# A recommender kernel's user stage: fixed rings of tiles, shorter lags and another order of the steps

## The chip, the cores and the metric

The kernel runs on one core of a Trainium2 chip. The time is that of one execution on the device, in microseconds (us). The profile is one such execution, recorded by the hardware profiler. TensorE (PE in the profile; its weight loads are PEld), VectorE (DVE), ScalarE (ACT), GpSimd (POOL) and SyncE (SP) each work through a queue of their own, in order.

## What is computed

Cut to what matters, the reference is:

```python
near_full = concat([near_pois, pad_row])              # 50001 items x 32 neighbours
def neighbor_attn(E):                                 # E: 50001 x 32
    V = E[near_full]                                  # gather
    w = softmax(einsum('nd,nkd->nk', E, V) / sqrt(32))
    return einsum('nk,nkd->nd', w, V)
a_sus, a_inf = neighbor_attn(E_in), neighbor_attn(E_out)
h = concat([E_hist[history], a_sus[history], a_inf[history]])   # 16384 x 100 x 128
t = concat([E_tgt[target],  a_inf[target],  a_sus[target]])     # 16384 x 128
z = relu(einsum('bld,hd->blh', h * t[:, None, :], W1) + b1)     # hidden size 128
exp_A = exp(einsum('blh,h->bl', z, W2[0])) * ((history != target) & (history != 0))
attn = exp_A / sqrt(sum(exp_A, -1))
s = sum(h * attn[..., None])                          # one number
out = sigmoid(dot / norms)                            # of s and t, for each of the 16384
```

## The kernel before

There are two long stages, one after the other.

The **neighbour stage** (lines 109 to 238) computes the two attentions for every item and writes one row of 129 numbers for each item into a table in HBM (`table`: the row's sum, then its 128 numbers), and one row of 128 into `ttab`. Its 12512 gathers are indirect DMAs issued by GpSimd at line 144. The diff does not touch it.

The **user stage** (lines 240 to 399) takes 128 chunks of 128 users each. A chunk has 100 history items per user, taken in groups of `LG = 4`, so `NG = 25` steps to a chunk and 3200 steps in all. The order of every engine's queue is the order of the program text; a framework puts in the semaphore waits that the data needs. An instruction can carry a wait of its own; where it needs a further one, a separate waiting instruction is put before it on that engine's queue. For step s:

- `gather(s)`, line 306, GpSimd: four indirect DMAs, each of which brings one row of 129 numbers for 128 users, into a tile `h`. There are `HBUF = 20` such tiles, so gathers run ahead of the work by up to 20 steps. The gather of step s + 20 must wait until TensorE and VectorE have read the tile of step s.
- `turn(s)`, line 320, TensorE: four transposes of 128x128 into one PSUM tile `hT_ps`, from a pool of three.
- `times_target(s)`, line 325, VectorE: multiplies that tile by the target's transposed row into `xT` (pool of six); line 328 copies the four row sums to `hsum`.
- `hidden(s)`, line 337, TensorE: one matmul with W1 (two passes in the profile) into `z_ps` (pool of three); line 339, ScalarE: bias and relu into `z` (pool of six).
- `scored(s)`, line 345, TensorE: one matmul (two passes) that adds the step's scores into `bank`, one PSUM tile for a chunk.

Once for each chunk there come `target_rows` (one gather, line 270), `target_work` (lines 282 to 297), `weights` (line 351), `exponents` (lines 358 and 360: four transposes into a tile of the same pool as `hT_ps`, and an Exp) and `ended` (lines 367 to 370).

The loop runs the steps with lags of `LAG = 3`. In iteration s the order is gather(s), turn(s), times_target(s), hidden(s-3), scored(s-6), and then the work of a chunk. Of PSUM's eight banks three go to `hT_ps`, three to `z_ps` and two to `bank`.

Of the kernel before, what the change touches and what calls it, by code (L numbers as in the profile page):

```python
# [10 lines left out]
F32 = mybir.dt.float32  # L11
# [3 lines left out]
AF = mybir.ActivationFunctionType  # L15
ALU = mybir.AluOpType
AX = mybir.AxisListType

P = 128
# [4 lines left out]
D = 128  # L24
# [22 lines left out]
LAG = 3  # L47
M = 2
HBUF = 20

# [3 lines left out]
def kernel(  # L54
# [194 lines left out]
    with (  # L249
# [12 lines left out]
        rows, got, hT, xT, z = {}, {}, {}, {}, {}  # L262
# [15 lines left out]
        def target_work(c):  # L278
            u = users[c]
            t = u["t"]  # L280
            tT_ps = ps_t.tile([P, LG, P], F32, name="hT_ps")
# [17 lines left out]
        def gather(s):  # L299
            c, g = divmod(s, NG)  # L300
            rows[s] = u_h.tile([P, LG, W], F32, name="h")
            got[s] = []
            for q in range(LG):
                l = g * LG + q
                got[s].append(
                    nc.gpsimd.indirect_dma_start(  # L306
                        out=rows[s][:, q, :],
                        out_offset=None,
                        in_=table,
                        in_offset=bass.IndirectOffsetOnAxis(  # L310
                            ap=users[c]["hidx"][:, l : l + 1], axis=0
                        ),
                    )
                )

        def turn(s):
            c, g = divmod(s, NG)
            hT[s] = ps_t.tile([P, LG, P], F32, name="hT_ps")
            for q in range(LG):
                nc.tensor.transpose(hT[s][:, q, :], rows[s][:, q, 1:W], ident)  # L320

        def times_target(s):
            c, g = divmod(s, NG)
            xT[s] = u_x.tile([D, LG, P], F32, name="xT")
            nc.vector.tensor_tensor(  # L325
                xT[s], hT.pop(s), users[c]["tT"].to_broadcast([D, LG, P]), ALU.mult
            )
# [4 lines left out]
            for one in got.pop(s):  # L332
                tc.declare_no_dep(copy.ins, one.ins, reason="TensorE has read the row")

        def hidden(s):
            z_ps = ps_z.tile([HID, LG, P], F32, name="z_ps")
            nc.tensor.matmul(z_ps, w1T, xT.pop(s), start=True, stop=True)  # L337
            z[s] = u_z.tile([HID, LG, P], F32, name="z")
            nc.scalar.activation(z[s], z_ps, AF.Relu, bias=b1_sb)  # L339

        def scored(s):
            c, g = divmod(s, NG)
            if g == 0:
                users[c]["bank"] = ps_s.tile([NG, LG, P], F32, name="bank")
            nc.tensor.matmul(  # L345
                users[c]["bank"], pick[:, g, :], z.pop(s), start=g == 0, stop=g == NG - 1
            )
# [6 lines left out]
        def exponents(c):  # L354
            flat = users[c].pop("flat")
            score = ps_t.tile([P, LG, P], F32, name="hT_ps")
# [20 lines left out]
        for s in range(last + 2 * LAG + 6):  # L377
            c, g = divmod(s, NG)
            if s < last:
# [107 lines left out]
```

## Time and profile before

| | us |
|---|---|
| median of 3 runs | 36161.68 (36157.8 to 36170.7) |
| the profiled execution | 36158.99 |
| its span, first to last instruction | 36157.2 |
| neighbour stage, to the first gather of the user stage | about 17540 |
| user stage, to its last gather | about 18550 |
| GpSimd busy | 25713.0 (71% of the span) |
| TensorE matmuls busy | 9955.5 (28%) |
| VectorE busy | 6910.6 (19%) |
| ScalarE busy | 2692.6 (7%) |

A row of a group of instructions reads: line, engine, operation, output <- inputs, shapes, count | busy us, mean ns of one | idle us of that engine just before them, and what ended the idle time. A row of a timeline reads: start us, length us, engine, line, operation, shapes, count, and in brackets the engine's idle time before it with what ended it.

### The profile page before, as it was taken

Reading aid. Unit: us, or ns where it says so; the run is one execution under the profiler, and the core shown is the slowest. Engines: PE = TensorE matmul, PEld = TensorE weight load, DVE = VectorE, ACT = ScalarE, POOL = GpSimd, SP = SyncE. Lnnn points to the kernel's source line nnn. Section 1 sums busy time; section 2 is a strip of 40 time slices with the busy share of each in tenths; the row PEclk is TensorE's granted clock in tenths of the full one; section 3 lists DMA queues with packets and bytes.
Section 4 is the critical chain, followed back from the end, with each engine's and each line's share of the span. In section 5 each row is a group of like instructions: output and inputs, shape, how many; then the busy total and the mean of one; then the engine's idle time right before and its main releaser. Section 6 shows DMA issues by size and latency. Waiting matters only on the chain.

```text
span 36157.2 us, 104181 instructions
## 1 busy us (share of the span) xinstructions
PE 9955.5 (28%) x26243; PEld 3219.9 (9%) x26243; DVE 6910.6 (19%) x9965; ACT 2692.6 (7%) x5700; POOL 25713.0 (71%) x25446
## 2 busy tenths in 40 slices
PE   0000000000000000000255555555555555555555
PEld 0000000000000000000011111111111111111111
DVE  2222222222222222222111111111111111111111
ACT  0000000000000000000011111111111111111111
POOL 7777777777777777777666666666666666666666
PEclk9999999999999999999877777777777777777777
DMA  1111111111111111111111111111111111111111
GB/s 42 29 27 27 27 28 29 27 27 27 28 29 28 27 27 28 27 29 25 40 47 47 47 47 47 47 46 47 47 47 47 46 47 46 47 47 47 46 46 43
DMA packets 1027956, 1362.32 MB, mean 38 GB/s; under 512 B 559904, under 2 KB 614432, under 8 KB 1027360
## 3 DMA queue, kind: packets, MB, share of 16 engines
q0 software_dynamic: 814080, 1265.42, 14.4%
q10 hardware_dynamic: 151056, 51.51, 0.8%
q1 hardware_dynamic: 62224, 38.72, 0.4%
q8 instruction: 218, 3.57, 0.0%
q14 instruction: 378, 3.10, 0.0%
HBM read 1315.31 MB, written 51.50 MB: 38 GB/s over the span
## 4 chain that ended last, share of the span: by engine, by line
POOL 37%; another core or an unknown queue 29%; PE 18%; issue 13%; DVE 2%; ACT 1%; DMA 0%; POOLq 0%; SPq 0%; ACTq 0%; DVEq 0%
POOL v L144 37%; PE z_ps L337 7%; PE bank L345 6%; PE hT_ps L320 5%; DVE xT L325 1%; ACT z L339 1%; DVE hsum L328 0%; DMA v<-in_egeo_dram,nidx 0%; PE hT_ps L358 0%; POOL h L306 0%; PE hT_ps L282 0%; ACT flat L351 0%; DVE tT L284 0%; DVE keep L293 0%
## 5 line engine op out<-in xcount | busy, mean ns | idle before, releaser
L306 POOL DMA_INDIRECT h<-table,hidx x12800 | 12107.2, 946 | 6300.4 <-issue 3830.4
L144 POOL DMA_INDIRECT v<-in_egeo_dram,nidx x12512 | 13484.1, 1078 | 4013.5 <-issue 3964.1
L325 DVE TENSOR_TENSOR xT<-hT_ps,tT 128x512 f32<-128x512 f32 x3200 | 2198.7, 690 | 15477.9 <-remote 9681.0
L282 PE MATMUL hT_ps<-ident,t 128*128 128x128 f32 x128 | 46.3, 362 | 17780.0 <-DMA t<-ttab,tidx 17522.1
L337 PE MATMUL z_ps<-xT,w1T 128*128 128x512 f32 x6400 | 4177.9, 741 | 1833.5 <-ACT z L339 1463.2
L320 PE MATMUL hT_ps<-ident,h 128*128 128x128 f32 x12800 | 2520.1, 328 | 5521.0 <-DVE xT L325 3984.9
L345 PE MATMUL bank<-z,pick 128*25 128x512 f32 x6400 | 3978.8, 709 | 0.0
L339 ACT ACTIVATE z<-z_ps,b_sb 128x512 f32<-128x512 f32 x3200 | 2149.8, 687 | 15996.4 <-remote 7924.9
L159 DVE TENSOR_TENSOR prod<-v,own_ps 128x4096 f32<-128x4096 f32 x196 | 864.4, 4410 | 12916.3 <-DMA v<-in_egeo_dram,nidx 12850.6
L320 PEld LDWEIGHTS hT_ps<-ident,h 128*128 128x128 f32 x12800 | 1621.4, 163 | 8660.4 <-DVE xT L325 4994.7
L282 PEld LDWEIGHTS hT_ps<-ident,t 128*128 128x128 f32 x128 | 19.1, 149 | 17919.3 <-issue 17586.5
L176 ACT ACTIVATE ex<-sc,top 128x32 f32<-128x32 f32 x782 | 227.8, 291 | 16993.6 <-DVE top L170 12332.7
L192 DVE TENSOR_TENSOR wv<-v,ex 128x1024 f32<-128x1024 f32 x782 | 1378.3, 1875 | 315.9 <-ACT ex L176 299.5
L337 PEld LDWEIGHTS z_ps<-xT,w1T 128*128 128x128 f32 x6400 | 1175.1, 230 | 2056.4 <-ACT z L339 1647.9
L166 DVE TENSOR_REDUCE sc<-prod 128x128 f32<-128x4096 f32 x196 | 864.4, 4410 | 6.7
L200 DVE TENSOR_REDUCE att<-wv 128x128 f32<-128x4096 f32 x196 | 864.1, 4409 | 6.0
L345 PEld LDWEIGHTS bank<-z,pick 128*25 128x25 f32 x6400 | 433.4, 109 | 3095.3 <-issue 3095.3
L328 DVE COPY hsum<-h 128x4 f32<-128x4 f32 x3200 | 568.9, 178 | 0.0
L358 PE MATMUL hT_ps<-ident,flat 25*128 25x25 f32 x512 | 65.8, 249 | 1051.5 <-ACT flat L351 714.5
L270 POOL DMA_INDIRECT t<-ttab,tidx x128 | 121.1, 946 | 65.9 <-issue 64.1
L358 PEld LDWEIGHTS hT_ps<-ident,flat 25*128 25x128 f32 x512 | 51.5, 170 | 1190.1 <-ACT flat L351 777.2
L176 ACT ACTIVATION_READ_ACCUMULATOR ex<-sc,top 128x1 f32 x782 | 146.0, 187 | 0.0
(55 smaller groups left out, 855.7 us busy)
## 6 DMA issues: line engine op xcount, KB each, us to landing
h<-table,hidx POOLq DMA_INDIRECT x12800
v<-in_egeo_dram,nidx POOLq DMA_INDIRECT x12512
table<-row ACTq DMA_DIRECT2D x22, 1096.5 KB
own<-in_egeo_dram SPq DMA_DIRECT2D x23, 544.0 KB
row<-in_ehist_dram SPq DMA_DIRECT2D x23, 544.0 KB
ttab<-in_etgt_dram ACTq DMA_DIRECT2D x1, 12500.0 KB
ttab<-row ACTq DMA_DIRECT2D x22, 544.0 KB
hidx<-in_history_dram SPq DMA_DIRECT2D x32, 200.0 KB
```

What stands on the lines that cost most here:

```text
L144: nc.gpsimd.indirect_dma_start(out=v[:, m, k].rearrange("p t d -> p (t d)"), out_offset=None, in_=egeo, in_offset=bass.IndirectOffsetOnAxi ...
L159: nc.vector.tensor_tensor(prod[:, 0:n].rearrange("p m k t d -> p m k (t d)"), v.rearrange("p m k t d -> p m k (t d)"), own_ps[:, 0:n].to_b ...
L166: nc.vector.tensor_reduce(sc[:, 0:n].rearrange("p m t k -> p m k t"), prod[:, 0:n], AX.X, ALU.add)
L192: nc.vector.tensor_tensor(wv[:, m, t].rearrange("p d k -> p k d"), subs[b]["v"][:, m, :, t, :], ex[:, m, t, :].rearrange("p (k o) -> p k o ...
L200: nc.vector.tensor_reduce(att[:, 0:n], wv[:, 0:n], AX.X, ALU.add)
L306: nc.gpsimd.indirect_dma_start(out=rows[s][:, q, :], out_offset=None, in_=table, in_offset=bass.IndirectOffsetOnAxis(ap=users[c]["hidx"][: ...
L320: nc.tensor.transpose(hT[s][:, q, :], rows[s][:, q, 1:W], ident)
L325: nc.vector.tensor_tensor(xT[s], hT.pop(s), users[c]["tT"].to_broadcast([D, LG, P]), ALU.mult)
L328: copy = nc.vector.tensor_copy(users[c]["hsum"][:, g * LG : (g + 1) * LG], rows.pop(s)[:, :, 0:1].rearrange("p q o -> p (q o)"),)
L337: nc.tensor.matmul(z_ps, w1T, xT.pop(s), start=True, stop=True)
L339: nc.scalar.activation(z[s], z_ps, AF.Relu, bias=b1_sb)
L345: nc.tensor.matmul(users[c]["bank"], pick[:, g, :], z.pop(s), start=g == 0, stop=g == NG - 1)
```

## The change

Only the user stage changes.

- The pools of `hT_ps`, `z_ps`, `xT` and `z`, from which each step took a tile, become lists of tiles that are allocated once and used in turn: `hT` has `TB = 2` (three before), `z_ps` has `ZP = 3` (three), `xT` has `XB = 4` (six), `z` has `ZB = 4` (six).
- The tile that `target_work` and `exponents` took from the pool of `hT_ps` comes from a pool of its own with one tile, `e_ps`.
- For two writes of one engine to the same tile of a ring, and for VectorE's read after the first three of the four transposes, the framework is told that no wait is needed (the engine's own order covers it, or the wait for the fourth transpose).
- The lags: hidden runs `LH = 2` steps behind turn (3 before), scored `LS = LH + ZP = 5` steps behind (6 before).
- The order in an iteration: gather(s), scored(s-5), hidden(s-2), turn(s), times_target(s), the work of a chunk.

The gathers, their 20 tiles, and the number and shapes of all matmuls, transposes and elementwise instructions stay as they are.

```diff
-LAG = 3
+TB = 2
+XB = 4
+ZP = 3
+ZB = 4
+LH = 2
+LS = LH + ZP
...
-        tc.tile_pool(name="u_x", bufs=6) as u_x,
-        tc.tile_pool(name="u_z", bufs=6) as u_z,
+        tc.tile_pool(name="u_r", bufs=1) as u_r,
...
-        tc.tile_pool(name="ps_t", bufs=3, space=bass.MemoryType.PSUM) as ps_t,
-        tc.tile_pool(name="ps_z", bufs=3, space=bass.MemoryType.PSUM) as ps_z,
+        tc.tile_pool(name="ps_r", bufs=1, space=bass.MemoryType.PSUM) as ps_r,
+        tc.tile_pool(name="ps_e", bufs=1, space=bass.MemoryType.PSUM) as ps_e,
...
+        hT = [ps_r.tile([P, LG, P], F32, name=f"hT{i}") for i in range(TB)]
+        z_ps = [ps_r.tile([HID, LG, P], F32, name=f"z_ps{i}") for i in range(ZP)]
+        xT = [u_r.tile([D, LG, P], F32, name=f"xT{i}") for i in range(XB)]
+        z = [u_r.tile([HID, LG, P], F32, name=f"z{i}") for i in range(ZB)]
+
+        def in_order(one, other):
+            tc.declare_no_dep(one.ins, other.ins, reason="one engine writes both in its order")
...
         def turn(s):
...
+                turned[s, q] = nc.tensor.transpose(
+                    hT[s % TB][:, q, :], rows[s][:, q, 1:W], ident
+                )
+                if s >= TB:
+                    in_order(turned[s, q], turned[s - TB, q])
...
         def times_target(s):
...
+            times[s] = nc.vector.tensor_tensor(
+                xT[s % XB], hT[s % TB], users[c]["tT"].to_broadcast([D, LG, P]), ALU.mult
+            )
+            for q in range(LG - 1):
+                tc.declare_no_dep(
+                    times[s].ins, turned[s, q].ins, reason="TensorE turns them in order"
+                )
+            if s >= XB:
+                in_order(times[s], times.pop(s - XB))
...
         def hidden(s):
+            first[s] = nc.tensor.matmul(
+                z_ps[s % ZP], w1T, xT[s % XB], start=True, stop=True
+            )
+            if s >= ZP:
+                in_order(first[s], first.pop(s - ZP))
+            second[s] = nc.scalar.activation(z[s % ZB], z_ps[s % ZP], AF.Relu, bias=b1_sb)
+            if s >= ZB:
+                in_order(second[s], second.pop(s - ZB))
...
-        for s in range(last + 2 * LAG + 6):
+        for s in range(last + LS + 6):
...
                 gather(s)
+            if 0 <= s - LS < last:
+                scored(s - LS)
+            if 0 <= s - LH < last:
+                hidden(s - LH)
+            if s < last:
                 turn(s)
                 times_target(s)
-            if 0 <= s - LAG < last:
-                hidden(s - LAG)
-            if 0 <= s - 2 * LAG < last:
-                scored(s - 2 * LAG)
...
-            done, left = divmod(s - 2 * LAG - NG, NG)
+            done, left = divmod(s - LS - NG, NG)
```

More of the change, by code (lines that the diff above doesn't have):

```diff
@@ L261 @@
         users, hists = {}, {}
-        rows, got, hT, xT, z = {}, {}, {}, {}, {}
+        got, turned, times, first, second = {}, {}, {}, {}, {}
+        rows = {}
+        hT = [ps_r.tile([P, LG, P], F32, name=f"hT{i}") for i in range(TB)]
[4 more added lines that the diff above has]
+            tc.declare_no_dep(one.ins, other.ins, reason="one engine writes both in its order")
         def history_of(i):
@@ L280, in target_work @@
             t = u["t"]
-            tT_ps = ps_t.tile([P, LG, P], F32, name="hT_ps")
+            tT_ps = ps_e.tile([P, LG, P], F32, name="e_ps")
             nc.tensor.transpose(tT_ps[:, 0, :], t, ident)
@@ L331, in times_target @@
             )
-            for one in got.pop(s):
-                tc.declare_no_dep(copy.ins, one.ins, reason="TensorE has read the row")
+            for q in range(LG):
+                tc.declare_no_dep(
+                    copy.ins, got.pop((s, q)).ins, reason="TensorE has read the row"
+                )
         def hidden(s):
[L336 to L339, printed above, removed]
+            first[s] = nc.tensor.matmul(
[6 more added lines that the diff above has]
+                in_order(second[s], second.pop(s - ZB))
         def scored(s):
@@ L345, in scored @@
             nc.tensor.matmul(
-                users[c]["bank"], pick[:, g, :], z.pop(s), start=g == 0, stop=g == NG - 1
+                users[c]["bank"], pick[:, g, :], z[s % ZB], start=g == 0, stop=g == NG - 1
             )
@@ L355, in exponents @@
             flat = users[c].pop("flat")
-            score = ps_t.tile([P, LG, P], F32, name="hT_ps")
+            score = ps_e.tile([P, LG, P], F32, name="e_ps")
             for q in range(LG):
```

23 lines of the change are left out of this document (7 added, 16 removed).

## The prediction

> **What bounds the kernel now.** I read the page first: its span, the chain that ended last and the costliest groups.
>
> ```profile
> span 36157.2 us, 104181 instructions
> ...
> POOL 37%; another core or an unknown queue 29%; PE 18%; issue 13%; DVE 2%; ACT 1%; DMA 0%; POOLq 0%; SPq 0%; ACTq 0%; DVEq 0%
> ...
> L325 DVE TENSOR_TENSOR xT<-hT_ps,tT 128x512 f32<-128x512 f32 x3200 | 2198.7, 690 | 15477.9 <-remote 9681.0
> ...
> L337 PE MATMUL z_ps<-xT,w1T 128*128 128x512 f32 x6400 | 4177.9, 741 | 1833.5 <-ACT z L339 1463.2
> L320 PE MATMUL hT_ps<-ident,h 128*128 128x128 f32 x12800 | 2520.1, 328 | 5521.0 <-DVE xT L325 3984.9
> L345 PE MATMUL bank<-z,pick 128*25 128x512 f32 x6400 | 3978.8, 709 | 0.0
> ```
>
> In the user stage no compute engine is near full: TensorE's three groups sum to 10677 us, VectorE's multiplies to 2199 us, and this in a stage of some 18550 us. VectorE sat 15478 us before its multiplies, most of it for a releaser that the profile can't name, and TensorE sat 5521 us before its transposes, for VectorE. So I asked next what GpSimd does in that stage, by line and by tile.
>
> ```profile
> L306 POOL DMA_INDIRECT h<-table,hidx x12793 | 12100.6, 946 | 6294.7 <-issue 3828.5 <-PE hT_ps L320 1786.3 <-DMA h<-table,hidx 265.2
> ...
> L306 POOL DMA_INDIRECT h<-table,hidx x12793: 939/947/1037, 17539.7 to 36092.5; - x200
> ```
>
> The gathers run from 17539.7 to 36092.5, that is 18552.8 us, and only about 65 us of the span come after them. They set the stage's length: 12793 of them, and 127 of the target's rows. The timeline of GpSimd shows at what pace.
>
> ```profile
> 23541.99 0.95 POOL L306 DMA_INDIRECT h<-table,hidx  x1 [0.30 <-issue]
> 23549.27 0.95 POOL L306 DMA_INDIRECT h<-table,hidx  x1 [6.33 <-PE hT_ps L320]
> 23550.52 0.95 POOL L306 DMA_INDIRECT h<-table,hidx  x1 [0.30 <-DVE xT L325]
> ...
> 23593.16 0.95 POOL L306 DMA_INDIRECT h<-table,hidx  x1 [0.30 <-issue]
> 23601.38 0.94 POOL L306 DMA_INDIRECT h<-table,hidx  x1 [7.27 <-PE hT_ps L320]
> ...
> L306 POOL DMA_INDIRECT h<-table,hidx x28 | 26.5, 946 | 13.6 <-issue 7.3 <-PE hT_ps L320 5.4 <-DMA h<-table,hidx 0.6
> ...
> L306 POOL DMA_INDIRECT h<-table,hidx x36 | 34.1, 946 | 17.1 <-issue 8.7 <-PE hT_ps L320 7.2 <-DMA h<-table,hidx 0.6
> ```
>
> A gather starts every 1.25 us, 0.95 busy and 0.30 between, until all 20 tiles are full; then GpSimd stands for some 7 us until one is free. The last two rows count the gathers from one such pause to the next: 28 before the pause of 6.33 us, 36 (nine steps) before that of 7.27 us. In the whole stage the idle time beyond 0.30 us a gather is 6294.7 - 12793 x 0.30 = 2457 us; a pause exceeds 0.30 by 6.0 and 7.0 us here, so with 6.5 there are some 378 pauses, one in every 8.5 steps. Without any, the stage would be 2.4 ms shorter.
>
> Why the tiles come free late is seen on VectorE and TensorE in the cycle between these two pauses.
>
> ```profile
> 23547.76 0.69 DVE L325 TENSOR_TENSOR xT<-hT_ps,tT 128x512 f32<-128x512 f32 x1 [10.50 <-PE bank L345]
> 23548.44 0.68 DVE L325 TENSOR_TENSOR xT<-hT_ps,tT 128x512 f32<-128x512 f32 x1
> 23549.10 0.68 DVE L325 TENSOR_TENSOR xT<-hT_ps,tT 128x512 f32<-128x512 f32 x1
> 23549.77 0.68 DVE L325 TENSOR_TENSOR xT<-hT_ps,tT 128x512 f32<-128x512 f32 x1
> 23554.25 0.69 DVE L325 TENSOR_TENSOR xT<-hT_ps,tT 128x512 f32<-128x512 f32 x1 [3.71 <-PE hT_ps L320]
> 23556.86 0.69 DVE L325 TENSOR_TENSOR xT<-hT_ps,tT 128x512 f32<-128x512 f32 x1 [1.64 <-PE hT_ps L320]
> 23559.28 0.69 DVE L325 TENSOR_TENSOR xT<-hT_ps,tT 128x512 f32<-128x512 f32 x1 [1.56 <-PE hT_ps L320]
> 23568.30 0.69 DVE L325 TENSOR_TENSOR xT<-hT_ps,tT 128x512 f32<-128x512 f32 x1 [8.08 <-PE z_ps L337]
> 23587.90 0.69 DVE L325 TENSOR_TENSOR xT<-hT_ps,tT 128x512 f32<-128x512 f32 x1 [18.83 <-issue]
> 23599.87 0.69 DVE L325 TENSOR_TENSOR xT<-hT_ps,tT 128x512 f32<-128x512 f32 x1 [11.21 <-PE bank L345]
> ...
> 23548.51 1.12 PE L320 MATMUL hT_ps<-ident,h 128*128 128x128 f32 x4 [1.76 <-DVE xT L325]
> 23549.42 1.92 PE L337 MATMUL z_ps<-xT,w1T 128*128 128x512 f32 x2
> 23551.26 1.90 PE L345 MATMUL bank<-z,pick 128*25 128x512 f32 x2
> 23553.09 1.12 PE L320 MATMUL hT_ps<-ident,h 128*128 128x128 f32 x4
> 23554.00 1.26 PE L337 MATMUL z_ps<-xT,w1T 128*128 128x512 f32 x2
> 23555.19 1.04 PE L345 MATMUL bank<-z,pick 128*25 128x512 f32 x2
> ...
> 23558.58 0.65 PE L320 MATMUL hT_ps<-ident,h 128*128 128x128 f32 x4
> 23559.08 1.02 PE L337 MATMUL z_ps<-xT,w1T 128*128 128x512 f32 x2
> 23560.03 1.04 PE L345 MATMUL bank<-z,pick 128*25 128x512 f32 x2
> 23561.00 0.66 PE L320 MATMUL hT_ps<-ident,h 128*128 128x128 f32 x4
> 23563.42 0.66 PE L320 MATMUL hT_ps<-ident,h 128*128 128x128 f32 x4
> ```
>
> The cycle has a quick and a slow stretch. Up to 23559.28 a multiply starts as soon as its transposes end (turn at 23558.58 for 0.65 us, multiply at 23559.28). Then TensorE's completions reach VectorE late: the turn that ends at 23561.66 is used at 23568.30, the one that ends at 23564.08 at 23587.90, 24 us later. The next multiply comes at 23599.87, which is 5.76 us after GpSimd went silent (23593.16 + 0.95). In the cycle before, the first multiply came 4.82 us after the silence (23547.76, after 23542.94). So while gathers are issued TensorE's results are seen at about one step in 20 us, and when the issue stops they come through. What holds them up the trace doesn't show; that it goes with the gathers it does. Seven quick steps and two slow ones make the nine steps of the cycle.
>
> **The price of a pause.** From 28 to 36 gathers the silence before the first multiply grows from 4.82 to 5.76 us, about 0.118 us a gather: a backlog that is paid in any order of work. The rest belongs to the pause itself. Over the stage: 2457 us less 12920 x 0.118 = 932 us, or 2.5 us for each of 378 pauses. The ends: if the silence were all backlog, only the 1.5 us from multiply to gather, less 0.3, is the pause's own, 1.2 us; if none, 6.5. I take 2.5, for it agrees with the whole stage. So the change is worth what it does to the number of pauses, that is to the steps per cycle.
>
> **The ring of transposes, three tiles to two.** When a slow stretch ends, the first three multiplies (23547.76, 23548.44, 23549.10) take turns that TensorE had made before: its first new one starts at 23548.51. These are the ring's three tiles. With two there are two. And in the new order TensorE doesn't stand before a turn, but before hidden(s), which now needs the multiply and comes ahead of the turn. With the durations above: multiply s ends at 23548.45, hidden from 23548.51 to the next start 1.84 later, turn to 23551.47, third multiply at 23551.5; then scored (1.83), hidden at the higher clock (1.19) and turn (0.65), fourth multiply at 23554.98; then every 2.42 us, as from 23558.58 to 23561.00: 23557.40 and 23559.82. Before, seven multiplies were done by 23559.28; now six by 23559.82, if the quick stretch ends at the same time. I take that it does, since it goes with the gathers and not with TensorE's work: one quick step less.
>
> One step less frees four gathers fewer: the slow stretch is 5.0 us shorter, at 20 us a step a further 0.25 step, and so on: 1/(1 - 0.25) = 1.33 steps. 8.5 becomes 7.2 steps, 378 pauses become 444. 66 x 2.5 = **+165 us** (79 at 1.2, 429 at 6.5).
>
> The Trainium skill, Perfetto Trace Analysis, Optimization Strategy, says that a gap that repeats on an engine can mean too little SBUF or PSUM for the next tile. It speaks against shortening this ring. TensorE's 5521 us before its transposes, 3985 of them for VectorE's multiply, are such gaps, and the trace agrees; by the rule the ring costs time, as in the sum, and it names no amount.
>
> **The separate waits.** They are not among the busy instructions, so I bound them. On VectorE they can't cost time in a quick stretch: multiplies start 0.67 us apart there at a length of 0.68. ScalarE's relu isn't on this path while three z_ps tiles stay. On TensorE, scored at 23560.03 is followed by turn 0.97 later, while hidden is followed by scored after 0.95: some 0.02 us, 0.07 at most, against 2.42 a step. It counts only in the quick stretch, 6 x 0.07 = 0.4 us in 52. I take nothing. If a separate wait took a place among the completions that trickle, 17 to a step (eight weight loads, eight matmuls, one wait), the slow stretch would give 2.1 steps for 2, some 20 us in all, less than the 0.2% (72 us) that a measurement here can tell.
>
> **Order, xT and z rings, chunk tile.** xT of four is read two steps later by hidden, z of four three steps later by scored: slack of two and of one step against work of 0.69 us. The chunk's two uses of e_ps lie nine steps apart. Exponents follow the last scored by a little more TensorE work than before. All nothing. The gathers themselves, and the stage ahead, are as before. At the tail scored follows one step, 2.4 us, sooner.
>
> The sum is made on the profiled execution's own 36158.99 us (span 36157.2 and 1.8 around it; the median of the runs, 36161.68, is 2.7 above): + 165 + 0 - 2 gives 36322, with the 2.7 about **36325 us**.
>
> **The rivals.** *Not slower:* the quick stretch ends after so many completions, not after a time. Then seven steps are quick in either kernel, it only lasts longer, pauses stay 378, and the time is 36160. For it: every quick step puts the same number of completions into the line. Against: in this cycle the trickle begins ten gathers after GpSimd resumed, as long as a backlog that grows with gathers would need. It decides if a profile after shows seven quick steps. The Trainium skill, TensorE: Matmul & The Clock Gate, "The cost: per-tile semaphore tail", gives 26 ns for each completion signalled; by it transposes would never be seen late and the ring's length would cost nothing, the same 36160. The 24 us above speak against that rule here.
>
> *Faster:* the separate waits do belong to what clogs, and without them the quick stretch holds for one or two steps more. One step, the ring's loss paid: 8.5 + 1.33 = 9.8 steps, 326 pauses, -130 us: 36030; a second one 35930. Against: the bound above. For: three engines wait separately, and I see none of it.
>
> *Slower still:* TensorE stays at the lower clock after each slow stretch (1.92 us for a pair, not 1.02), since it now begins with one pair and a turn and waits again. Two quick steps go: 5.8 steps, 552 pauses, +435: 36595. For: pairs of 1.9 last until 23553 even with three turns in hand.
>
> *It doesn't do what it says:* the waits stay under another name; then the ring alone acts, which is the forecast.
>
> **How the numbers follow.** Forecast 0.42, not slower 0.22, faster 0.24, slower still 0.12. The forecast lies over the 72 us unless a pause costs 1.1 us or less, which I hold for unlikely. So faster by more than 0.2%: 0.25, within: 0.22, slower: 0.53. The range reaches from the faster case with one step, a little beyond, to the slower case: 36000 to 36600.
>
> **What would show it.** Right: GpSimd's idle time in the user stage rises by about 150 to 200 us; a cycle has 28 to 32 gathers; after a silence two multiplies start 0.7 apart and the third some 3 us later. Wrong: cycles of 36 gathers or more, or a gather pace other than 1.25 us. Matmul counts and lengths should not change.

## The result, and the profile after

| | before | after |
|---|---|---|
| median of 21 runs each | 36163.92 us | 36218.61 us |
| lowest to highest | 36136.88 to 36175.84 | 36200.41 to 36249.47 |
| profiled execution: span | 36157.2 us | 36207.1 us |
| its granted TensorE clock | 0.854 | 0.864 |

The changed kernel takes 1.0016 times as long, 95% interval 1.0009 to 1.0023: some 55 us slower. That is the side that the prediction took, at a third of its size (+165 us), and below the 72 us that it had set as the least that could be told; with 21 runs of each it could.

The page of the changed kernel: the span, and the groups that answer to those shown of before. GpSimd's gathers are L317 now, the transposes L328, the multiplication by the target L336, the two TensorE products L355 and L368.

```profile
span 36207.1 us, 98804 instructions
...
L317 POOL DMA_INDIRECT h<-table,hidx x12800 | 12076.4, 943 | 6387.1 <-issue 5175.1
...
L355 PE MATMUL z_ps<-xT,w1T 128*128 128x512 f32 x6400 | 4542.5, 798 | 8512.6 <-DVE xT L336 7742.9
L336 DVE TENSOR_TENSOR xT<-hT,tT 128x512 f32<-128x512 f32 x3200 | 2206.6, 691 | 15844.6 <-remote 10547.6
...
L368 PE MATMUL bank<-z,pick 128*25 128x512 f32 x6400 | 3896.7, 695 | 0.3 <-ACT z L360 0.3
...
L328 PE MATMUL hT<-ident,h 128*128 128x128 f32 x12800 | 2357.2, 316 | 16.9 <-DMA h<-table,hidx 16.6
```

The waiting instructions are gone: 104181 instructions have become 98804. TensorE's wait for VectorE has moved, as the order says it must, from the transposes (5521.0 us before, 16.9 after) to the first product (1833.5 before, 8512.6 after). It doesn't set the time. GpSimd's row does; its counterpart, from the same view of the groups by line of the kernel before with all 12800 gathers, is this one.

```profile
L306 POOL DMA_INDIRECT h<-table,hidx x12800 | 12107.2, 946 | 6300.4 <-issue 3830.4 <-PE hT_ps L320 1786.3 <-DMA h<-table,hidx 265.2
```

GpSimd's idle time rose by 6387.1 - 6300.4 = 87 us and its busy time fell by 31 us. The last gather ends 3 us nearer to the span's end (60.5 us, 63.7 before) and the first starts 2 us sooner, so the span grew by 50 us. One cycle, from silence to silence, shows where the idle time comes from. In the timeline (start, length, instruction, and in brackets the idle time before it with what ended it) stand first the two gathers before which GpSimd was silent, then VectorE's multiplications and some of TensorE's work in the same 47 us.

```profile
23541.80 0.94 POOL L317 DMA_INDIRECT h<-table,hidx  x1 [6.87 <-issue]
...
23588.34 0.94 POOL L317 DMA_INDIRECT h<-table,hidx  x1 [6.91 <-issue]
...
23540.29 0.69 DVE L336 TENSOR_TENSOR xT<-hT,tT 128x512 f32<-128x512 f32 x1 [12.57 <-remote]
23540.97 0.68 DVE L336 TENSOR_TENSOR xT<-hT,tT 128x512 f32<-128x512 f32 x1
23544.00 0.69 DVE L336 TENSOR_TENSOR xT<-hT,tT 128x512 f32<-128x512 f32 x1 [1.17 <-PE hT L328]
23547.09 0.69 DVE L336 TENSOR_TENSOR xT<-hT,tT 128x512 f32<-128x512 f32 x1 [2.32 <-issue]
23549.55 0.69 DVE L336 TENSOR_TENSOR xT<-hT,tT 128x512 f32<-128x512 f32 x1 [1.70 <-PE hT L328]
23552.01 0.69 DVE L336 TENSOR_TENSOR xT<-hT,tT 128x512 f32<-128x512 f32 x1 [1.69 <-PE z_ps L355]
23558.73 0.69 DVE L336 TENSOR_TENSOR xT<-hT,tT 128x512 f32<-128x512 f32 x1 [5.95 <-PE bank L368]
23572.81 0.69 DVE L336 TENSOR_TENSOR xT<-hT,tT 128x512 f32<-128x512 f32 x1 [13.31 <-remote]
23586.83 0.69 DVE L336 TENSOR_TENSOR xT<-hT,tT 128x512 f32<-128x512 f32 x1 [13.26 <-remote]
...
23541.04 2.08 PE L355 MATMUL z_ps<-xT,w1T 128*128 128x512 f32 x2 [8.87 <-DVE xT L336]
23542.91 1.06 PE L328 MATMUL hT<-ident,h 128*128 128x128 f32 x4
...
23545.49 1.13 PE L355 MATMUL z_ps<-xT,w1T 128*128 128x512 f32 x2
23546.45 0.60 PE L328 MATMUL hT<-ident,h 128*128 128x128 f32 x4
...
23556.30 0.60 PE L328 MATMUL hT<-ident,h 128*128 128x128 f32 x4
```

The gathers between the two silences, as one group of the lines of that window:

```profile
L317 POOL DMA_INDIRECT h<-table,hidx x32 | 30.2, 943 | 16.3 <-issue 14.2 <-PE hT L328 0.6 <-DMA h<-table,hidx 0.6
```

After the silence two multiplications start 0.68 us apart, the third 3.03 us later, the fourth 3.1 us after that and the next two at 2.5 us each: six quick ones up to 23552.01. Two slow ones follow at 23558.73 and 23572.81. The turn that ends at 23556.90 is used at 23572.81, 16 us late. Eight steps, 32 gathers: one quick step less than in the cycle of before, close to the places worked out.

For the whole stage I counted the cycles in the trace: from one silence of GpSimd of more than 1.5 us to the next, silences within 15 us of each other taken together, between 18.0 and 36.0 ms. Before there are 352 cycles with 8.8 steps (35.6 gathers), most often nine; after there are 409 with 7.6 steps (30.6 gathers), most often eight. A silence, beyond the usual 0.30 us, became shorter: 5.8 us in place of 6.5. So 57 cycles more cost 87 us of idle time: **some 1.5 us each, not 2.5**.

### The profile page after: what moved, and what is told of

Read it like the earlier page. It is cut to its first block, busy times and chain, and to the rows that moved or that the text cites. A ratio compares the mean times of both kernels' runs of the same rounds, so it can differ in the third digit from the quotient of the medians.

```text
span 36207.1 us, 98804 instructions
## 1 busy us (share of the span) xinstructions
PE 9945.0 (27%) x26243; PEld 3633.9 (10%) x26243; DVE 6951.2 (19%) x9965; ACT 2744.3 (8%) x5700; POOL 25679.2 (71%) x25446
## 4 chain that ended last, share of the span: by engine, by line
POOL 32%; another core or an unknown queue 30%; PE 17%; issue 17%; DVE 3%; DMA 0%; ACT 0%; SPq 0%; POOLq 0%; ACTq 0%
POOL v L149 32%; PE z_ps L355 8%; PE bank L368 6%; PE hT L328 3%; DVE xT L336 3%; DMA v<-in_egeo_dram,nidx 0%; DVE hsum L345 0%; PE e_ps L381 0%; POOL h L317 0%; DVE keep L306 0%; ACT z L360 0%; PE e_ps L295 0%; DVE tT L297 0%; DVE ea L392 0%
## 5 line engine op out<-in xcount | busy, mean ns | idle before, releaser
L317 POOL DMA_INDIRECT h<-table,hidx x12800 | 12076.4, 943 | 6387.1 <-issue 5175.1
L355 PE MATMUL z_ps<-xT,w1T 128*128 128x512 f32 x6400 | 4542.5, 798 | 8512.6 <-DVE xT L336 7742.9
L336 DVE TENSOR_TENSOR xT<-hT,tT 128x512 f32<-128x512 f32 x3200 | 2206.6, 691 | 15844.6 <-remote 10547.6
L368 PE MATMUL bank<-z,pick 128*25 128x512 f32 x6400 | 3896.7, 695 | 0.3 <-ACT z L360 0.3
L328 PE MATMUL hT<-ident,h 128*128 128x128 f32 x12800 | 2357.2, 316 | 16.9 <-DMA h<-table,hidx 16.6
L355 PEld LDWEIGHTS z_ps<-xT,w1T 128*128 128x128 f32 x6400 | 1167.9, 229 | 11831.9 <-DVE xT L336 9316.1
L328 PEld LDWEIGHTS hT<-ident,h 128*128 128x128 f32 x12800 | 1965.1, 167 | 2308.1 <-issue 2213.4
L368 PEld LDWEIGHTS bank<-z,pick 128*25 128x25 f32 x6400 | 434.1, 109 | 667.1 <-issue 544.2
L162 ACT COPY own_ps<-own 128x64 f32<-128x64 f32 x391 | 82.3, 210 | 57.1 <-issue 49.4
```

What stands on the lines that cost most here:

```text
L317: got[s, q] = nc.gpsimd.indirect_dma_start(out=rows[s][:, q, :], out_offset=None, in_=table, in_offset=bass.IndirectOffsetOnAxis(ap=users[ ...
L328: turned[s, q] = nc.tensor.transpose(hT[s % TB][:, q, :], rows[s][:, q, 1:W], ident)
L336: times[s] = nc.vector.tensor_tensor(xT[s % XB], hT[s % TB], users[c]["tT"].to_broadcast([D, LG, P]), ALU.mult)
L355: first[s] = nc.tensor.matmul(z_ps[s % ZP], w1T, xT[s % XB], start=True, stop=True)
L368: nc.tensor.matmul(users[c]["bank"], pick[:, g, :], z[s % ZB], start=g == 0, stop=g == NG - 1)
```

## The experiments

All changed the user stage alone. A ratio is to the kernel before as it ran beside the kernel named, on the same chip; by its medians before took 36173 to 36266 us there, and 31897 us on the one chip named below. "Step" is four gathers and what follows from them.

**Which edit shortens the cycles.** Four kernels on one chip: the ring of transposes alone, the changed kernel with its waits, the order and lags alone, and the changed kernel with three transposed tiles.

```diff
 # before, the ring alone
-ps_t = tile_pool(name="ps_t", bufs=3)
+ps_t = tile_pool(name="ps_t", bufs=2)   # target's and exponents' tiles in a pool ps_e of one
```

> The kernel before with the ring of transposed tiles at two in place of three (the target's and the exponents' tiles in a tile of their own), its old order, its lags of 3 and 6 and all its separate waits kept. Theory (the ring of two ends the quick stretch one step sooner, and an extra pause costs some 1.4 us): about 409 cycles of 31 gathers, 8 steps the commonest length, some 60 more pauses than before, and a time 60 to 110 us above the kernel before; the part above the 55 us of the changed kernel would be the gathers' 3 ns (12800 x 0.0026 = 33 us), if the other edits brought that. Rival (the new order or the lags make the cycles shorter, not the ring): cycles of 35.6 gathers as before, and a time within 20 us of the kernel before.

```diff
 # after, the waits back
-            tc.declare_no_dep(one.ins, other.ins, ...)   # in_order, and that of times_target on turned
+            return
```

> The changed kernel with its declarations on the rings left out, so that TensorE, VectorE and ScalarE issue the separate waiting instructions again (some 5000 more instructions); rings, lags and order as in the changed kernel. Theory (separate waits cost nothing here, GpSimd's pauses decide): the time of the changed kernel, 45 to 65 us above the kernel before, with cycles of 31 gathers. Rival (leaving out the waits bought back part of the ring's price, by shorter gathers or shorter pauses): 85 to 120 us above the kernel before, gathers again 946 ns.

```diff
 # before, order and lags alone; ps_t stays at 3
-turn(s); times_target(s); hidden(s - 3); scored(s - 6)
+scored(s - 5); hidden(s - 2); turn(s); times_target(s)
```

> The kernel before with the new order of the loop and the lags of 2 and 5, but with three tiles in the ring of transposed tiles, its pools and its separate waits kept. With a lag of two the first multiply of step s-2 stands ahead of the transposes of step s on TensorE and waits for VectorE's multiplication of step s-2, so TensorE can run no more than two steps ahead of VectorE, however many tiles the ring has. Theory (the run-ahead is what ends the quick stretch): cycles of 31 gathers as in the changed kernel, and 45 to 90 us above the kernel before. Rival (the tiles of the ring themselves decide): cycles of 35 to 36 gathers, and within 20 us of the kernel before.

```diff
 # after
-TB = 2; ZP = 3; LH = 2
+TB = 3; ZP = 2; LH = 3
```

> The changed kernel with three tiles in the ring of transposed tiles, a lag of 3 for the first multiply and two z_ps tiles (there are eight banks), its order and its declarations kept, so without separate waits. Theory (run-ahead of three steps gives the old cycles, separate waits cost nothing): cycles of 35 to 36 gathers, and within 25 us of the kernel before; if the 3 ns shorter gathers come with the waits left out, 20 to 45 us below it. Rival (the new order or the ring of z_ps decides): cycles of 31 gathers or fewer, and 45 us or more above the kernel before.

| kernel | tiles: transposes / z_ps, lag of hidden | separate waits | cycles, steps in one | ratio, 95% interval |
|---|---|---|---|---|
| before (first pair) | 3 / 3, 3 | yes | 352, 8.8 | 1 |
| after (first pair) | 2 / 3, 2 | no | 409, 7.6 | 1.0016, 1.0009 to 1.0023 |
| ring of two alone | 2 / 3, 3 | yes | 419, 7.3 | 1.0024, 1.0014 to 1.0033 |
| waits back | 2 / 3, 2 | yes | 425, 7.2 | 1.0019, 1.0010 to 1.0028 |
| order, ring of three | 3 / 3, 2 | yes | 438, 7.0 | 1.0025, 1.0015 to 1.0034 |
| no waits, ring of three | 3 / 2, 3 | no | 397, 7.8 | 1.0005, 0.9996 to 1.0014 |

The ring of two by itself makes the time longer (+80 us by the medians), and its cycles are short: its rival, within 20 us of before, falls. The order and the lag do the same with three tiles (+91 us): a lag of two holds TensorE two steps from VectorE whatever the ring has. With the waits put back it is +76 us, between the 45 to 65 of the theory and the 85 to 120 of its rival, and no further from the changed kernel than the intervals leave open. The last kernel came out within 25 us of before as expected (+13), but with cycles of 31.4 gathers where 35 to 36 were expected; it has only two z_ps tiles, which a later run takes up.

The times in the table can be compared more safely than the cycles. On this chip the kernel before took some 100 us longer than in the first pair, and no trace of it was taken there, so how many cycles it had beside these four isn't known. The same holds for the z_ps kernels below.

The groups by line, GpSimd's row of the ring alone, of the waits back and of the order alone, in this order. They hold nearly the same idle time, 6488 to 6534 us.

```profile
L307 POOL DMA_INDIRECT h<-table,hidx x12800 | 12095.7, 945 | 6487.8 <-issue 3860.5 <-PE hT_ps L321 2314.2 <-remote 97.9
```

```profile
L317 POOL DMA_INDIRECT h<-table,hidx x12800 | 12076.3, 943 | 6496.0 <-issue 5330.0 <-remote 875.0 <-PE hT L328 121.5
```

```profile
L307 POOL DMA_INDIRECT h<-table,hidx x12800 | 12076.4, 943 | 6534.2 <-issue 5333.9 <-remote 901.5 <-PE hT_ps L321 152.1
```

**Pacing the gathers.** If the silences are a backlog being worked off, gathers issued more slowly leave none. A fill on GpSimd behind each gather does that.

```diff
                 got[s].append(nc.gpsimd.indirect_dma_start(...))
+                nc.gpsimd.memset(spare, 0.0)   # spare: 128 x 1, or 128 x 128, or wider
```

> The kernel before with one more GpSimd instruction behind each of the 12800 gathers of the user stage: it fills a spare tile of 128 x 1 with zeros (GpSimd's fills of that size took 98 to 118 ns in the profile of before), which nothing reads. Theory (gathers issued every 1.25 us are issued faster than they are worked off; the backlog of some 0.12 us per gather holds up TensorE's completions, and the pauses are the time in which it is worked off, so that a cycle costs 1.37 us per gather and 2.4 us of its own): the gathers stand some 1.35 us apart, the pauses become few (under 120 in place of 352 cycles) or vanish, TensorE's completions come at once for most steps, and the stage takes 12928 x 1.36 to 1.40 = 17580 to 18100 us in place of 18567, so 450 to 950 us below the kernel before. Rival (the pauses do not come from the gathers' pace, they are a fixed cost per step): every gather is 0.1 us later and the pauses stay, 800 to 1300 us above the kernel before. Second rival (the fill is hidden in the 0.30 us between two gathers): no change of pace, within 50 us of the kernel before.

> The same with a spare tile of 128 x 128 (one such fill took 205 ns in the profile of before). Theory: gathers 1.45 us apart, slower than they are worked off at 1.37 to 1.40 us, no pauses, every completion at once, and the stage takes 12928 x 1.45 = 18750 us, some 180 us above the kernel before; if a fill costs less than 205 ns at the margin, correspondingly less. Rival (pauses are a fixed cost): 2600 us above the kernel before. Second rival (hidden between two gathers): within 50 us.

> The changed kernel with 40 in place of 20 h tiles, so that GpSimd can run 40 steps ahead. Theory (the pauses are the time in which a backlog of gathers is worked off, and the h tiles only set how large it grows): at first GpSimd runs on for longer, but TensorE's steps come at the pace at which its completions come, so cycles and time stay as in the changed kernel, within 40 us of it (15 to 95 us above the kernel before). Rival (GpSimd pauses because it has too few tiles, and more of them cover the slow stretch): fewer and longer cycles, 200 us or more below the changed kernel.

> The changed kernel with the short fill of 128 x 1 behind each gather. Theory (where the backlog does not build up, nobody waits for the ring of transposed tiles): the same time as the kernel before with that fill, within 30 us, and 450 to 950 us below the kernel before. Rival (the ring of two costs by itself): 50 us or more above the kernel before with the fill.

These four met the chip on which the kernel before takes 31897 us. With the short fill: 1.0036 (1.0023 to 1.0049), with the longer one 1.0369 (1.0353 to 1.0385), forty tiles in the changed kernel 1.0012 (1.0003 to 1.0021), the changed kernel with the short fill 1.0036 (1.0023 to 1.0050). The groups by line of before with the short fill show another picture.

```profile
L307 POOL DMA_INDIRECT h<-table,hidx x12800 | 12082.6, 944 | 2575.4 <-issue 2350.5 <-PE hT_ps L322 123.7 <-PE bank L347 75.9
...
L316 POOL MEMSET spare<- 128x1 f32 x12800 | 1505.2, 118 | 4.0
...
L327 DVE TENSOR_TENSOR xT<-hT_ps,tT 128x512 f32<-128x512 f32 x3200 | 2213.1, 692 | 13184.4 <-PE hT_ps L322 13181.5
```

GpSimd's idle is 2575 us: some 0.19 us between a fill and the next gather, and 123 longer gaps, about one every 106 gathers, that make 117 us together. The silences of 6 us are not there. Those gaps are as much as the kernel takes above before (115 us); what they are the trace doesn't show. So the second rival had the pace right and the time not. VectorE waits for its transposes and for nothing else: from the end of a turn to its multiplication it took 37 to 39 ns in 98 of 100 steps. The short fill lay within the 0.30 us between two gathers (but for those gaps they still start 1.25 us apart), the longer one put them 1.334 us apart. So nothing here could tell of a backlog: there was none to take away. But this chip tests something else. With the short fill, before and after take 32012.49 and 32012.54 us: where completions come at once, the ring of two costs nothing.

The next four met a chip on which before takes 36175 us.

> The changed kernel, unaltered, beside the kernel before on the chip of this call; two chips have been seen so far, one on which the kernel before takes 36160 to 36270 us and one on which it takes 31897 us and every completion of TensorE reaches VectorE within 39 ns. Theory (the ring of two costs where completions come late, and nowhere else): 45 to 90 us above the kernel before on a chip of the first kind, within 10 us of it on one of the second, with a lag of 37 to 39 ns there. Rival (the ring, the order or the lags cost by themselves): 45 us or more above on both kinds.

> The kernel before with a GpSimd fill of a spare 128 x 128 tile behind each gather, which spaced the gathers 1.334 us apart where nothing else held them. On a chip on which before takes 36200 us, theory (a backlog of 1.37 to 1.40 less the pitch per gather): the backlog grows by 0.04 to 0.07 us per gather in place of 0.12 to 0.15, cycles two to three times as long, GpSimd's pauses total under 1200 us, and the time 300 to 700 us below the kernel before. Rival (a step costs its pauses whatever the pitch): 800 us or more above. On a chip on which before takes 31900 us: 1175 us above, as seen there.

> The kernel before with a fill of a spare 128 x 192 tile behind each gather; by the fills of 128 x 1 and 128 x 128 (118 and 221 ns) the gathers stand some 1.385 us apart. On a chip on which before takes 36200 us, theory: hardly any backlog, fewer than 100 pauses, most completions within 0.2 us, and the stage takes 12928 x 1.385 = 17905 us plus what pauses are left, 400 to 660 us below the kernel before. Rival (a step costs its pauses whatever the pitch): 1500 us or more above. On a chip on which before takes 31900 us: 1750 to 1900 us above, by the pitch alone.

> The changed kernel with 40 h tiles. On a chip on which before takes 36200 us, theory (the tiles only set how large the backlog grows, and what ends is the pace at which it is worked off): within 60 us of the changed kernel of this call. Rival (too few tiles make GpSimd pause): 200 us or more below it. On a chip on which before takes 31900 us: some 40 us above the kernel before, as seen there.

The changed kernel again: 1.0010 (1.0001 to 1.0020), +36 us by the medians, below the 45 expected, with 410 cycles of 7.6 steps. Before, paced at 1.33 us: 0.9974 (0.9964 to 0.9984), -88 us; at 1.39 us: 0.9946 (0.9930 to 0.9963), -195 us. The rival (a step costs its pauses whatever the pitch) wanted at least 800 and 1500 us more and falls; the size expected, 300 to 700 and 400 to 660 us, was too large, as the next runs explain. Forty tiles: 1.0024 (1.0014 to 1.0034), 53 us above the changed kernel beside it, and nearly the same idle time:

```profile
L317 POOL DMA_INDIRECT h<-table,hidx x12800 | 12080.7, 944 | 6388.3 <-issue 5451.9 <-remote 658.5 <-PE hT L328 117.5
```

Twice the tiles buy nothing: the cycles are those of the changed kernel (407 of 7.6 steps). Of the 53 us, 46 come after the last gather (115.9 us to the span's end in place of 70.3), with 40 multiplications left to do in place of 20.

**The floor.** The last question was why a cycle costs so little.

```diff
 # before, TensorE's and its followers' work left out
-            turn(s)
-            hidden(s - LAG); scored(s - 2 * LAG); weights(done); exponents(done)
-            xT[s] = ...; nc.vector.tensor_tensor(xT[s], hT.pop(s), ...)
```

> The kernel before with all of the user stage's work on TensorE and ScalarE's work behind it left out (transposes, both multiplications, the weights and their sum; the score is then made of the stored row sums alone): GpSimd gathers into 20 h tiles, VectorE copies the row sums and frees the tiles. On a chip on which before takes 36200 us, theory (a floor of 1.40 us per gather, the settled pace of the first stage; what before takes above it, 18562 - 12928 x 1.40 = 463 us or 1.3 us for each of 352 cycles, is what the late completions cost): gathers 1.40 us apart in the middle of the stage, 18080 to 18150 us for the stage, 400 to 490 us below the kernel before. Rival (there is no floor above 1.25 us, the pauses are wholly TensorE's late completions): 16150 us for the stage, 2400 us below. Second rival (the floor is 1.43 to 1.44 us): within 120 us of the kernel before.

> The kernel before with a fill of a spare 128 x 214 tile behind each gather, some 1.41 us apart. On a chip on which before takes 36200 us, theory (floor of 1.40 us per gather): the pauses total under 200 us, most completions come within 0.2 us, and the stage takes 12928 x 1.41 = 18230 us plus those, 200 to 340 us below the kernel before and 20 to 150 us below the one paced at 1.39. Rival (no floor, late completions stay whatever the pitch): pauses as with 1.39, slower than that kernel by 12928 x 0.02 = 260 us.

```diff
-ps_t bufs=3, ps_z bufs=3
+ps_t bufs=4, ps_z bufs=2
```

> The kernel before with four tiles in the ring of transposed tiles and two z_ps tiles, nothing else changed. On a chip on which before takes 36200 us, theory (one more quick step per cycle, and a cycle costs 1.3 us above the floor): 9 to 11 steps per cycle, 290 to 325 cycles in place of 352, 30 to 90 us below the kernel before. Rival (2.5 us a cycle, as first forecast): 90 to 160 us below. Second rival (something other than the ring ends the quick stretch from three on): cycles of 8.8 steps, within 20 us.

> The ring of four with a fill of a spare 128 x 204 tile behind each gather, some 1.40 us apart. On a chip on which before takes 36200 us, theory: few pauses, the stage near 12928 x 1.405 = 18164 us plus under 150 us, 250 to 400 us below the kernel before and below every kernel so far. Rival (pacing and a longer ring buy the same thing): within 30 us of the kernel paced at 1.39 or 1.41, the better of them. On a chip on which before takes 31900 us: 1900 us above it, by the pitch alone.

Gathers alone: 0.9851 (0.9834 to 0.9867), -545 us, a little more than expected, since the tail has gone as well. GpSimd's row in 1400 us of it, from 24000 to 25400 us, by line:

```profile
L296 POOL DMA_INDIRECT h<-table,hidx x991 | 1053.3, 1063 | 334.8 <-issue 311.1 <-DMA h<-table,hidx 23.6
L265 POOL DMA_INDIRECT t<-ttab,tidx x10 | 10.4, 1045 | 3.1 <-issue 3.1
```

1001 gathers in 1400 us: 1.40 us each, with none of the stage's TensorE work. The stage took 18070 us. And the number had been there all along: in the kernel before, by line from 12000 to 13400 us, in the stage ahead, whose gathers have nothing to wait for but themselves:

```profile
L144 POOL DMA_INDIRECT v<-in_egeo_dram,nidx x1001 | 1081.3, 1080 | 320.0 <-issue 316.3 <-DMA v<-in_egeo_dram,nidx 3.7
```

On the chip with the 31897 us the same 1400 us hold 1120 gathers, 1.25 us each (forty tiles, same view):

```profile
L149 POOL DMA_INDIRECT v<-in_egeo_dram,nidx x1120 | 1056.8, 944 | 344.1 <-issue 335.8 <-DMA v<-in_egeo_dram,nidx 8.4
```

So where gathers settle at 1.40 us, 12928 of them take some 12928 x 1.40 = 18099 us whatever TensorE does (18070 with gathers alone). The stage of before, first gather to last, is 18562.5 us: all that stands above the floor is 463 us, 1.3 us for each of 352 cycles. After it is 18617.5 us, 518 us over 409 cycles, again 1.3. The other unpaced kernels give 1.2 to 1.3 where before takes about 36170 us, and 1.4 to 1.6 where it takes about 36260; what makes that difference isn't shown.

This floor is a pace of issuing, not of moving data. The trace's DMA packets (32 for a gather, in the gathers' order) show no backlog of transfers: in the user stage of before the last packet of a gather ends 1.2 us after its instruction, 1.3 us at the 95th of 100, and 1.3 and 1.4 on the chip with the 31897 us. With gathers alone VectorE read a step 0.45 us after its last packet, in the median, at the settled pace too. So the backlog spoken of here is not one of transfers; the last section has what the trace shows of it.

Paced at 1.41 us: 0.9920 (0.9904 to 0.9937), -296 us, the fastest whole kernel of all. Its gathers, by line:

```profile
L307 POOL DMA_INDIRECT h<-table,hidx x12800 | 12172.3, 951 | 2261.2 <-issue 1985.1 <-PE hT_ps L322 96.5 <-PE z_ps L339 53.9
L316 POOL MEMSET spare<- 128x214 f32 x12800 | 3763.1, 294 | 7.8
```

The idle time is 2261 us in place of 6300, the cycles 49 in place of 352, and some 30 of these are gaps at every 106th gather, as on the other chip. One expectation failed: most completions still came late, 11 us in the median. The tiles last all the same. That nothing more piles up would explain it; it isn't shown.

The ring of four missed: 1.0013 (1.0004 to 1.0023), slower, with 8.0 steps in a cycle where 9 to 11 were expected. Paced at 1.40 us it gives 0.9940 (0.9924 to 0.9957), -219 us, between the two paced at 1.39 and 1.41 us without it. What the theory had overlooked is that this kernel has two z_ps tiles, so I tried those by themselves, and then everything of the change with three and three.

```diff
 # before                         # after
-ps_z bufs=3                     -TB = 2; LH = 2
+ps_z bufs=2                     +TB = 3; LH = 3   # target's and exponents' transposes in the next z_ps tile
```

> The kernel before with two z_ps tiles in place of three, nothing else changed: the first multiply of step s-3 then waits for ScalarE's reading of step s-5, and that for TensorE's completion two steps back. On a chip on which before takes 36200 us, theory (TensorE's run-ahead over the engines that wait for its completions is that of its smallest PSUM ring, whichever it is): 7.0 to 8.0 steps per cycle as in all kernels with a two in either place, and 35 to 80 us above the kernel before. Rival (only the ring of transposed tiles or the lag of the first multiply counts): 8.5 to 9 steps per cycle and within 20 us of the kernel before.

> The changed kernel (its order, fixed tiles and declarations, so no separate waits) with three tiles in the ring of transposed tiles and a lag of 3; three z_ps tiles as there, and the target's and the exponents' transposes in the next free z_ps tile, since there are eight banks. On a chip on which before takes 36200 us, theory (the shorter ring was the whole price of the change, and a cycle loses 1.35 us above the floor): 8.5 to 9.2 steps per cycle, about 350 cycles, and within 20 us of the kernel before, on the lower side if leaving the waits out is worth anything. Rival (the new order costs by itself): 45 us or more above. Second rival (the separate waits had a price that the ring hid): 30 us or more below.

Two z_ps tiles alone: 1.0013 (1.0004 to 1.0022), +46 us, 388 cycles of 7.9 steps, as expected and as with the ring of four: ScalarE needs TensorE's completions no less than VectorE does, and the smaller of the two rings would decide. The kernel without waits, with two z_ps tiles as well, came out at +13 us, with an interval that reaches to 51; so the size of this is loose. Three and three without waits: 1.0004 (0.9995 to 1.0014), +13 us, no difference that can be told from the kernel before, so neither rival (45 us above, 30 us below) holds. But its cycles were 387 with 8.0 steps, spread widely, not the 8.5 to 9.2 expected: as many as with two z_ps tiles alone, in 33 us less. So the count of cycles doesn't give the time by itself. What shortens some of them stays open.

## Why the prediction was right and wrong

**What bounds the kernel** was right: the gathers set the stage's length, GpSimd's silences come from TensorE's completions arriving late, and what the changed kernel lost is in GpSimd's idle row. That they are late only where gathers settle at 1.40 us is seen on the other chip: there 98 of 100 turns are used within 39 ns. That the gathers are the cause was not shown, and the two chips may differ in more.

**The ring costs one quick step** was right, and nearly in number: on the first pair 8.8 steps became 7.6 where 8.5 to 7.2 was forecast, 57 more cycles were counted where 66 were forecast, the multiplications stand where the working put them (0.68 and 3.03 us after the silence). The ring alone costs as much or more (+80 us). That the lag of two would do it with three tiles as well the prediction said only in passing (hidden ahead of the turn); it is a second cause of about the same size (+91 us), and the two together are not more (+36 to +76 us). That the count came out near without this cause weighed is in part luck. (The forecast's 444 pauses are 3200 steps by 7.2, its 378 are 2457 us by 6.5; on one footing the difference is 68, not 66, or 5 us.)

**The price of a pause** is the step that failed: the 2.5 us. It took the backlog as 0.118 us a gather, from two silences (4.82 and 5.76 us), which is 1525 us in the stage, and so left 2457 - 1525 = 932 us to the pauses themselves. The backlog of a gather is what the floor leaves over the pitch, 1.400 - 1.251 = 0.149 us; 12928 of them are 1926 us, and 2457 - 1926 = 531 us over 378 pauses are 1.4 us each. It also fits the two silences: 28 and 36 gathers make 4.2 and 5.4 us of the 4.82 and 5.76, so that nearly all of each silence is backlog. The 1.251 and the 1.400 were both to be had from the trace of before, the latter from the first stage. With 1.4 us, 66 pauses would have given +92 us, and the 57 counted ones +80. The lower end that the prediction named, 1.2 us, was nearer than the value it took; "it agrees with the whole stage" was no evidence, since the same 0.118 stood on both sides.

**The rest of the difference**, -31 us, is the gather itself: 946 ns in the profile of before, 943 in that of after. That the change did this is not shown: 943 ns are also measured in the ring of four and with two z_ps tiles, which keep the old order and all waits, and 945 in the second profile of the changed kernel.

**The separate waits at nothing** stands, within what was measured: put back, 1.0019 (1.0010 to 1.0028) against 1.0016 and 1.0010 without them, though not side by side. A price of up to some 40 us is not excluded. The rival "faster" (the waits clog) falls, since without them the time rose and the cycles became shorter. "Not slower" (so many completions, not so long a time) falls with the six quick steps. "Slower still" (the clock) falls too: the first product after the silence took 2.08 us, the next at 23545.49 already 1.13, and there were 409 cycles, not 552.

The Trainium skill, Perfetto Trace Analysis, Optimization Strategy, says that a gap repeating on the engine that should be saturated can mean too little SBUF or PSUM for the next tile. For both PSUM rings the times agree (+80 us and +46 us for one tile less), though the gaps read for it were TensorE's, which is not the engine that sets the time; for SBUF they don't, where twenty more h tiles won nothing. The Trainium skill, TensorE: Matmul & The Clock Gate, "The cost: per-tile semaphore tail", gives some 26 ns for each completion signalled. Delays of that order are what the one chip shows (37 to 39 ns from a turn's end to its use, which is not the same quantity); the others are far from it (16 us in the cycle shown).

## What to carry to other kernels

Before pricing a pause, look for the pace at which the paused engine's work is served when nothing else holds it, in another stage if need be: only the time above that floor can be won or lost, and here it was 463 us where the idle row showed 2457. Where an engine's completions come late, look at all rings and lags between it and every consumer together: here one tile less in either PSUM ring, or a lag of two, cost 46 to 91 us each, and two of them together no more. This kernel gained from issuing gathers at their settled pace (-296 us), but only on a chip that is slow in this: the 128 x 128 fill cost 1175 us where gathers ran at 1.25 us.

## What the runs showed of the hardware

- The kernel before took 36137 to 36285 us on the other chips and 31894 to 31902 us on one. Most of the difference is the pace of gathers issued by GpSimd: 1.400 us each when settled, against 1.25 us, which over 25440 gathers is some 3800 us; the 463 us above the floor are the rest. Why chips differ the runs don't show.
- TensorE's completions reached VectorE with a median delay of 7.2 us in the kernel before (34 us at the 95th of 100), and in 37 to 39 ns on that other chip. On the slower chips the delay was there at every pace of the gathers tried, from 1.25 to 1.41 us (11 us in the median at 1.41).
- It is TensorE's completions that are late, not all. In the changed kernel TensorE's first product started 53 to 55 ns after VectorE's multiplication in every one of 1123 waits of more than 0.5 us.
- TensorE's late completions come through one after another on a grid. The trace has times at which a semaphore was raised, not all but most. Of the intervals of more than 0.5 us between raises of TensorE's semaphore in the user stage, 71% lie within 0.03 us of a multiple of 0.70 us in the kernel before and 69% in the changed one, where chance would give 9%; on the other chip, with the short fill, 4% do. 0.70 us is half the settled 1.40 us of a gather. In the silence that begins at 23594.11 in the kernel before, four are 4.2, 0.71 and 0.70 us apart, and then come sixteen from 23599.81 to 23600.38, 0.03 to 0.05 us apart. It looks like a queue that moves at this pace until it is empty; what serves it no trace shows.
- A fill on GpSimd of 128 x 1 (118 ns) behind a gather cost no pitch: it lay in the 0.30 us that GpSimd leaves between two gathers. With it came a longer gap about every 106 gathers, 117 us in all. One of 128 x 128 (221 ns) added 0.085 us.
